# Cross attention with fast 3x3 products: setup reordered, and the last batch's softmax steps moved between engines

## The chip, the cores and the metric

The kernel runs on one core of one Trainium2 chip. The metric is the device time of one execution in microseconds. TensorE (PE in the profile) multiplies into PSUM; VectorE (DVE), ScalarE (ACT) and GpSimd (POOL) work elementwise, and only the first two of these read PSUM. SyncE (SP) issues most of the transfers. The engines run their own instruction streams, in the order that the kernel writes, and wait for one another by semaphores.

## The reference

There are 16 batches of 100 queries with 640 features, and 722 context rows of 384 features each. The first 718 rows are ordinary keys and values; the last 4 (tokens) take part in a second attention. Everything is float32 and has 8 heads of 80 features.

```python
query = hidden_states @ Wq
keyt = enc @ Wk
valt = enc @ Wv
hs = _mha(query, keyt, valt)
ca_q1 = jnp.einsum('btc,th->bch', ca, Wq_ca)[:, indices, :]
ca_hs1 = _mha(ca_q1, residual, residual)
ca_q2 = ca_hs1 @ Wq
ca_hs2 = _mha(ca_q2, ca @ Wk_ca, ca @ Wv_ca)
out = (hs + ca_hs2) @ Wout + b_out + residual
```

`_mha` scales its scores by 1/sqrt(80), takes the softmax over the keys and multiplies with the values.

## The kernel before

**Products of thirds.** The 718 keys of a batch are cut into three thirds of 240 columns (KT; two of 120, KN, for the values) and the 384 features into three channel blocks of 128 (CC). Keys and values are not made with 27 block products but with 15, from sums of encoder blocks (`enc_sums`, on GpSimd) and sums of weight blocks (`weight_sums`, twelve subtractions each for Wk and for Wv). `V_PLAN` and `K_PLAN` list the 15 products in order: the PSUM bank that takes it, its form, and the place in the result to which the bank is then added. The first bank that goes to a place is copied there by ScalarE (L412), each later one added by VectorE (L410). `go(n)` issues the next n products with their copies and adds. The last batch uses `END_PLAN`, the same products in another order.

**Setup.** Batch 0 has no earlier batch beside which its keys could be made, so `first_keys` makes them with plain products (L626): four chunks of keys times three thirds times three channel blocks, 36 products, each of which is two instructions in the profile. Ahead of them, five products on zeros (L1263) run while the first loads are under way. The weights of the keys arrive transposed (`load_heads`, L302 and L309) and are turned back by TensorE (`turn_back`, L589) and copied to `wk_sb` by VectorE or ScalarE (L592): chunks 0 and 1 at once, 2, 3 and 4 after the first four groups of products. Behind the first keys follow, in TensorE's order: the token keys k_ps (L1295), five groups of m_ps (L1319), which fold Wq into the token keys, the first queries q_ps (L544), y_ps (L805), the last chunk of the keys (L568), the other queries, and the token values va_ps (L1362). Then the loop over the batches begins with the scores s_ps (L666).

VectorE in the setup copies turned-back weights (L592), reduces a mask (L1266), makes seven of Wk's sums, all twelve of Wv's, the five late ones of Wk (these overwrite blocks of Wk that the first keys read), and then multiplies the token keys by a mask into `k2T` (L1307), which m_ps reads. It copies each group of m_ps to `m_sb` (L1327). GpSimd multiplies those by another mask (`keys`, L777) for y_ps.

**Loads.** The loads of the setup go through SyncE's queue and, for a few, ScalarE's. An issue waits until an earlier transfer has landed whose semaphore it uses again; there are eight such semaphores, taken in turn. Behind the encoder blocks stand the token loads (L319, L320), Wv (L322), Wq transposed (L326), the queries' input (L328), Wq (L333), the tokens' sample (L335) and the encoder tile of batch 1 (L248, L261).

**A batch.** A batch makes its scores in three tiles st 0, 1 and 2, each copied from PSUM by ScalarE (L688, L694), and a running maximum over the keys by VectorE (`larger`, L1403, L1412). `Maximum` turns this into one value per query and head in steps (`top.go`): transpose, reduce, four small reductions and their merge, a spread by ScalarE (L751), a transpose back (`over`, L759). `subtract` takes it from each st tile, `exponential` (L1399) follows on ScalarE. The rows of ones beside the values give the sums r_ps (L1543); a_ps (L1561) gives the values' part. The second attention runs beside it: `softmax2` (z_ps), `scores2` (three small steps on VectorE and an exponential on ScalarE), `softmax3` (two steps on VectorE, one on GpSimd), `spread2` (a transpose on VectorE, then transfers by way of DRAM: four stores L919, one widened copy L924, loads L929 and L933), and `values2` (seven steps on GpSimd, L943 and L947) with the sum `hs2`. `divide`, `place` and `finish` scale and add, and `project...` multiplies with Wout.

**The last batch.** The branch `else` of the loop body orders the last batch by hand. `last` is the batch before it, whose last full output block is projected in two halves: the first half's product early, with its sum into `xn` and its store kept back in `due` until `put()`, the second behind r_ps. r_ps reads the st tiles in the order 1, 2, 0, 1, 0, 2. The tail is `project_last` (L1225), its sum (L1234) and its store.

Of the kernel before, what the change touches and what calls it, by code (L numbers as in the profile page):

```python
# [14 lines left out]
B, S, H = 16, 100, 640  # L15
# [5 lines left out]
CC = CAD // P  # L21

KT = SK // 3 + 1
# [36 lines left out]
for h in range(NH):  # L60
    lo = h * D
    while lo < (h + 1) * D:
        c = lo // P
# [84 lines left out]
def kernel(  # L148
# [117 lines left out]
    def a_raw(enc, u, c):  # L266
        if (u, c) in A_REST:
            return enc[1][:, A_REST[u, c]]
        return enc[0][:, A_RAW[u, c]]
# [20 lines left out]
    wkt_sb = kT.rearrange("p c u k -> p c (u k)")[:, :, :CAD]  # L290
    enc = enc_tile("enc_0"), rest_tile("rest_0")

    def load_first(queue, u, lo, hi):
        to = a_raw(enc, u, lo) if hi == lo + 1 else enc[0][:, A_RAW[u, lo] :][:, : hi - lo]
        queue.dma_start(
            out=to,
            in_=enct[0][:, slice(lo, hi) if hi > lo + 1 else lo, u * (KT - 1) : u * (KT - 1) + KT],
        )

    def load_heads(u):  # L300
# [1 line left out]
            (nc.scalar, nc.sync)[h // 2 % 2].dma_start(**packed(wkt_sb, wkt, h))  # L302

    load_heads(0)
    load_first(nc.sync, 0, 0, 3)
    load_first(nc.scalar, 1, 0, 1)
    load_first(nc.sync, 1, 1, 3)
    load_heads(1)
    nc.sync.dma_start(  # L309
        out=wkt_sb[:, 4], in_=wkt.rearrange("(h k) n -> h k n", h=NH)[:, 64:]  # L310
    )
    load_first(nc.sync, 2, 0, 2)
    load_first(nc.sync, 2, 2, 3)
    tokens = pb_tile("tokens")
    beside = wide("beside")[:, : CC * (B * T + P)]
    cat_sb = beside[:, : CC * B * T].rearrange("p (c n) -> p c n", c=CC)
# [191 lines left out]
            begun = begun or first  # L508
        return begun

    def weight_sums(engine, w, late=None):

        at = lambda f: w[:, W_AT[f]]
        raw = lambda c, g: w[:, 2 * (c - 1) + g - 1]
        sums = (
            (0, raw(1, 2), raw(1, 1)),
            (11, raw(2, 2), raw(3, 2)),
            (12, raw(3, 2), raw(3, 1)),
            (5, raw(2, 2), raw(1, 2)),
            (7, raw(3, 2), at(5)),  # L520
            (13, raw(3, 1), at(7)),
            (1, raw(2, 1), raw(3, 1)),
            (3, raw(1, 1), at(7)),
            (6, raw(2, 1), raw(1, 1)),
            (10, raw(3, 1), raw(2, 2)),
            (2, raw(1, 1), raw(2, 2)),
            (14, raw(2, 1), raw(2, 2)),
        )
        for f, left, right in sums:
            if late is None or late == (f in (5, 7, 13, 3, 14)):  # L530
                engine.tensor_tensor(at(f), left, right, ALU.subtract)

# [64 lines left out]
    def first_keys(enc):  # L597

        banks = {}
        copies = nc.scalar.copy, nc.vector.tensor_copy  # L600

        def begin(n, get):
            if get is pair:
                both = pair(f"kT_ps_0_{n}")
                banks[n] = [both[:, k] for k in range(2)]
            else:
                banks[n] = [get(f"kT_ps_0_{n}_{k}") for k in range(2)]

        for n in range(2):
            turn_back(n, nc.vector.tensor_copy)  # L610
            begin(n, pair)
        for u, chunks in (
            (0, (0, 1)),
            (1, (0, 1)),
            (0, (2, 3)),
            (1, (2, 3)),
            (2, range(4)),
        ):
            if len(banks) < 4 and 2 in chunks:
                for n in (2, 3, 4):  # L620
                    turn_back(n, copies[n % 2])
                begin(2, psum1)
                begin(3, psumk)
            for n in chunks:
                for c in range(CC):
                    nc.tensor.matmul(  # L626
                        banks[n][u // 2][:, u % 2 * KT : (u % 2 + 1) * KT],
                        wk_sb[:, 2 * c + n % 2, n // 2],
                        a_raw(enc, u, c),
                        start=(u != 1 and c == 0),  # L630
                        stop=(c == CC - 1),
                        skip_group_check=True,
                    )
        for n in banks:
            for bank, thirds in zip(banks[n], ((0, 1), (2,))):
                w = len(thirds)
                nc.scalar.copy(
                    kT[:, n, thirds[0] : thirds[0] + w],
                    bank[:, : w * KT].rearrange("p (u k) -> p u k", u=w),
                )  # L640
# [618 lines left out]
    idle = vaT[:, :2].rearrange("p c n -> p (c n)")  # L1259
    nc.vector.memset(idle, 0.0)  # L1260
    idle_ps = psum("idle_ps")
    for _ in range(5):
        nc.tensor.matmul(idle_ps[:, :P], idle, idle, start=True, stop=True)  # L1263

    first_keys(enc)
# [3 lines left out]
    nc.gpsimd.memset(most[96:, :], LOW)  # L1269
    nc.gpsimd.memset(e1[96:, :], LOW)  # L1270
    weight_sums(nc.vector, wk_sb, False)
    weight_sums(nc.vector, wv_sb)
    weight_sums(nc.vector, wk_sb, True)
    enc_sums(enc)

# [40 lines left out]
    for c in range(HC):  # L1316
        m_ps = psum(f"m_ps_{c}")
        for n, heads in enumerate(HEADS):
            nc.tensor.matmul(  # L1319
                m_ps[:, heads[0] * B * T : (heads[-1] + 1) * B * T],  # L1320
                wqt_sb[:, n, c * P : (c + 1) * P],
                k2T[n],
                start=(n == 0),
                stop=(n == HC - 1),
                skip_group_check=True,
            )
        nc.vector.tensor_copy(  # L1327
            m_sb[c].rearrange("p (b h t) -> p h b t", h=NH, t=T),
            m_ps.rearrange("p (h b t) -> p h b t", h=NH, b=B),
        )  # L1330
        nc.sync.dma_start(out=m_d[c], in_=m_sb[c])
    nc.sync.dma_start(out=wvca_sb, in_=wvca.rearrange("(c p) n -> p c n", p=P))
    second = Second(0, xT, ca_0)
    keys(load_m(0))
# [38 lines left out]
    for b in range(B):  # L1373
# [16 lines left out]
        def subtract(i, engine=nc.vector):  # L1390
            return engine.tensor_tensor(  # L1391
                st[i],
                st[i],
                top.over[:KN].unsqueeze(1).to_broadcast([KN, 2, ROWS]),
                ALU.subtract,
            )
# [26 lines left out]
        if b + 1 < B:  # L1423
            second.products()
            second.copy()
        if b == B - 1:
            now.scores2()
        seen = larger(2)
        top = Maximum(most, f"{b}", True)

        if b + 1 < B:

            def both(n):
                vv.go(n)
                kk.go(n)

            if waiting:
                wait_for(enc_sums(enc, LATE_SUMS), seen)
            if waiting:
                second.scores1(tokens=range(T - 1))  # L1440
            else:
                second.scores1(seen)
            store(seen)
            if last:
                last.load(seen)
            if b == B - 2:
                again()
            if b + 2 < B:
                m_next = load_m(b + 2, seen)
            if b == 1:  # L1450
                load_outputs(nc.sync.dma_start, wout_sb, wout)
            top.go(3)
            both(3)
            now.scores2()
            top.go(1)
            both(2)
            top.go()
            both(2)
            now.softmax3()
            if waiting:  # L1460
                second.scores1(tokens=range(T - 1, T))
            if b + 2 < B:
                keys(m_next)
            both(1)
            now.spread2()
            vv.go(2)
            kk.go(1)
            subtract(0)
            exponential(0)
            vv.go(1)  # L1470
            less = subtract(1)
            if last:
                last.place(less)
                if last.b in PAIRED:
                    last.row_sums()
                last.add_bias()
            if b == B - 2:
                mine.load(seen)
            now.values2()
            if b == B - 2:  # L1480
                mine.add_bias()
            vv.go(1)
            kk.go(2)
            exponential(1)
            vv.go(1)
            kk.go(2)
            both(1)
            both(1)
            if b == 1:
                nc.gpsimd.dma_start(out=bias, in_=bout[0].partition_broadcast(P))  # L1490
            second_next, enc_next = loads()
            subtract(2)
            exponential(2)
            last_keys(b + 1, enc)
            if b + 2 < B:
                enc_next = load_rest(b + 2, enc_next)
        else:
            last.place()
            mine.load(seen)
            now.softmax3()  # L1500
            top.go(1)
            now.spread2()
            top.go(2)
            vv.go(3)
            last.project_few(len(OC) - 2)
            last.project((0,), True, put=False)
            top.go(1)
            top.go()
            vv.go(2)
            less = subtract(0)  # L1510
            exponential(0)
            wait_for(subtract(2, nc.gpsimd), less)
            vv.go(3)
            last.put()
            vv.go(1)
            now.values2(subtract(1))
            mine.add_bias()
            exponential(2)
            vv.go(1)
            exponential(1)  # L1520
            vv.go(5)
        paired = last and last.b in PAIRED
        late = b % 2 == 0 and not paired
        if b < B - 1 and (b % 2 or late):
# [106 lines left out]
```

## Time and profile before

| | before |
|---|---|
| median of 3 runs | 929.62 us (929.5 to 931.77) |
| profiled execution | 931.78 us |
| its span, first to last instruction | 930.1 us |
| PE busy | 916.3 us (99%) |
| DVE busy | 672.0 us (72%) |
| POOL busy | 616.1 us (66%) |
| ACT busy | 375.5 us (40%) |

The profiled execution's own time is 1.7 us more than its span, for what lies around the first and the last instruction. Busy time of PE counts pipelined matmuls, so 99% does not say that the array is at its peak. In a row of the order of time stand: start and length in us, engine, line, operation, output and inputs, shapes, how many instructions are merged, and in brackets the idle time before them with what ended it. In a row by windows: the stretch, its length, the busy time and count of PE, PEld, DVE, ACT and POOL, the granted TensorE clock, the DMA share and GB/s. In a row of waits: who waited for whom, the total in us, how often, and the longest.

### The profile page before, as it was taken

What the parts mean: (1) busy time and instruction counts of PE and PEld (TensorE: products, weight loads), DVE (VectorE), ACT (ScalarE), POOL (GpSimd) and SP (SyncE); (2) the same over time, 40 slices, a digit from 0 to 9 for tenths busy, and PEclk for the clock granted to TensorE, in tenths of its full rate; (3) what the DMA queues carried; (4) which work ended last, traced back from release to release, by engine and by line L of the source; (5) the groups of instructions that cost most, each with busy time, mean ns of one, the idle gap of its engine ahead of it and who ended that gap; (6) DMA issues with size and microseconds to landing.
All of it is one profiled execution on the core that took longest, in us unless ns stands there. A gap on an engine that the chain in (4) does not pass through costs nothing.

```text
span 930.1 us, 26065 instructions
## 1 busy us (share of the span) xinstructions
PE 916.3 (99%) x11151; PEld 781.3 (84%) x11151; DVE 672.0 (72%) x1122; ACT 375.5 (40%) x654; POOL 616.1 (66%) x652
## 2 busy tenths in 40 slices
PE   8899999999999999999999999999999999999998
PEld 7798979888888888888798887988888888888865
DVE  3699796887828787585966759669792887828783
ACT  1344443444424354542435324344541444415341
POOL 7455798566955778477574766846796566955623
PEclk9899999999999999999999999999999999999999
DMA  9412253051401504131141401304140141401331
GB/s 304 157 45 61 84 121 86 6 133 42 109 11 34 140 6 109 44 96 46 34 109 43 123 20 49 93 15 132 43 109 9 35 135 40 109 11 45 85 83 32
DMA packets 67997, 69.50 MB, mean 75 GB/s; under 512 B 25129, under 2 KB 61289, under 8 KB 67881
## 3 DMA queue, kind: packets, MB, share of 16 engines
q1 hardware_dynamic: 66952, 66.97, 26.8%
q8 instruction: 88, 1.44, 0.6%
q10 hardware_dynamic: 464, 0.52, 0.2%
q0 software_dynamic: 464, 0.34, 0.2%
q14 instruction: 29, 0.23, 0.1%
HBM read 62.14 MB, written 8.94 MB: 76 GB/s over the span
## 4 chain that ended last, share of the span: by engine, by line
PE 96%; DVE 2%; DMA 1%; issue 0%; POOL 0%; ACT 0%; SPq 0%; DVEq 0%
PE s_ps L666 12%; PE v_psA L439 11%; PE v_psB L439 9%; PE k_psA L470 8%; PE a_ps L1561 7%; PE q_ps L544 7%; PE k_psB L470 7%; PE kT_ps L568 6%; PE r_ps L1543 4%; PE v_psC L439 3%; PE k_psC L470 3%; PE y_ps L805 2%; PE v_psD L439 2%; PE v_psE L439 2%; PE o_psy L1134 2%; PE k_psE L470 1%
## 5 line engine op out<-in xcount | busy, mean ns | idle before, releaser
L840 POOL TENSOR_TENSOR e<-ca,g 100x800 f32<-100x800 f32 x60 | 91.7, 1539 | 102.1 <-DVE most L1403 87.9
L439 PE MATMUL v_psA<-wv_sb,enc 128*120 128x320 f32 x384 | 119.7, 434 | 0.7 <-ACT vs L412 0.7
L507 POOL TENSOR_TENSOR enc<-enc 128x240 f32<-128x240 f32 x144 | 111.6, 784 | 8.0
L439 PE MATMUL v_psB<-wv_sb,enc 128*120 128x320 f32 x320 | 99.2, 433 | 0.0
L666 PE MATMUL s_ps<-qp,kT 32*120 32x100 f32 x3072 | 97.5, 263 | 0.0
L666 PEld LDWEIGHTS s_ps<-qp,kT 32*120 32x120 f32 x3072 | 94.7, 180 | 1.9
L847 POOL TENSOR_TENSOR e<-e,e 100x800 f32<-100x800 f32 x45 | 92.1, 2047 | 3.5
L1391 DVE TENSOR_TENSOR st<-st,over 120x1600 f32<-120x1600 f32 x47 | 91.4, 1945 | 0.0
L439 PEld LDWEIGHTS v_psA<-wv_sb,enc 128*120 128x120 f32 x384 | 69.1, 184 | 25.6 <-ACT vs L412 1.2
L470 PE MATMUL k_psA<-enc,wk_sb 128*128 128x240 f32 x360 | 87.7, 366 | 0.0
L470 PEld LDWEIGHTS k_psA<-enc,wk_sb 128*128 128x128 f32 x360 | 68.6, 190 | 17.0
L1403 DVE TENSOR_TENSOR most<-most,st 120x800 f32<-120x800 f32 x64 | 63.5, 991 | 22.6 <-ACT st L688 21.5
L439 PEld LDWEIGHTS v_psB<-wv_sb,enc 128*120 128x120 f32 x320 | 58.7, 183 | 23.2
L1399 ACT ACTIVATE st<-st 120x1600 f32<-120x1600 f32 x48 | 73.9, 1540 | 7.2 <-DVE st L1391 5.2
L470 PE MATMUL k_psB<-enc,wk_sb 128*128 128x240 f32 x300 | 73.1, 366 | 0.0
L1412 DVE TENSOR_TENSOR most<-st 120x800 f32<-120x800 f32 x16 | 17.2, 1074 | 76.0 <-ACT st L694 76.0
L1561 PE MATMUL a_ps<-st,vs 120*64 120x100 f32 (+1 forms) x1536 | 69.5, 250 | 0.0
L544 PE MATMUL q_ps<-xT,wq_sb 128*128 128x200 f32 x400 | 69.1, 333 | 0.0
L1561 PEld LDWEIGHTS a_ps<-st,vs 120*64 120x64 f32 (+1 forms) x1536 | 66.4, 137 | 2.7 <-issue 2.6
L544 PEld LDWEIGHTS q_ps<-xT,wq_sb 128*128 128x128 f32 x400 | 68.0, 190 | 0.2
L412 ACT COPY vs<-v_psA 120x640 f32<-120x640 f32 x48 | 33.2, 693 | 84.4 <-PE v_psA L439 84.3
L694 ACT COPY st<-s_ps 120x800 f32<-120x800 f32 x64 | 49.7, 829 | 43.4 <-PE s_ps L666 43.4
(183 smaller groups left out, 1890.6 us busy)
## 6 DMA issues: line engine op xcount, KB each, us to landing
pb<-p_d SPq DMA_DIRECT2D x32, 400.0 KB
enc<-in_enct SPq DMA_DIRECT2D x32, 240.0 KB
enc<-in_enct SPq DMA_DIRECT2D x16, 360.0 KB
xT<-in_xt SPq DMA_DIRECT2D x8, 500.0 KB
rest<-in_enct SPq DMA_DIRECT2D x31, 120.0 KB
xn<-in_x SPq DMA_DIRECT2D x11, 320.0 KB
wide_d<-p_d SPq DMA_DIRECT2D x16, 200.0 KB
pb<-wide_d SPq DMA_DIRECT2D x16, 200.0 KB
```

The lines of the kernel that those rows point to most:

```text
L439: nc.tensor.matmul(at[0][j][:KN, : H // 2], a_form(self.enc, f)[:, j * KN : (j + 1) * KN], wv_sb[:, W_AT[f]], start=first, stop=last, skip ...
L470: nc.tensor.matmul(at[:, i * KT : (i + 1) * KT], wk_sb[:, W_AT[f], i], a_form(self.enc, f), start=(first and i == 0), stop=last, skip_grou ...
L507: first = nc.gpsimd.tensor_tensor(out, left, right, op)
L544: nc.tensor.matmul(q_ps[:, : 2 * S].rearrange("p (j s) -> p j s", j=2), wq_sb[:, c, n * P : (n + 1) * P], xT[:, :, c, :], start=(c == 0), ...
L568: nc.tensor.matmul(bank[:, i * KT : (i + 1) * KT], weights[c], a_raw(enc, u, c), start=(i == 0 and c == 0), stop=(c == CC - 1), skip_group ...
L666: nc.tensor.matmul(s_ps[bank][:n, 256 * a + lo : 256 * a + lo + rhs.shape[-1]], kT[rows, c, u, j * KN : (j + 1) * KN], rhs, start=bank not ...
L840: first = engine.tensor_tensor(to, self.ca[:, t, :].unsqueeze(1).to_broadcast([S, NH, S]), g[:, :, t].unsqueeze(2).to_broadcast([S, NH, S] ...
L847: engine.tensor_tensor(e, e, to, ALU.add)
L1391: return engine.tensor_tensor(st[i], st[i], top.over[:KN].unsqueeze(1).to_broadcast([KN, 2, ROWS]), ALU.subtract,)
L1399: nc.scalar.activation(st[i], st[i], AF.Exp, scale=SCALE)
L1403: most_now = nc.vector.tensor_tensor(most[:KN], most[:KN], st[i][:, u], ALU.max)
L1561: nc.tensor.matmul(wides[64 * e : 64 * e + 64, h // 2], slot(i, h, FIRST[e], 64), st[i // 2][: KEYS[i], i % 2, h * S : (h + 1) * S], start ...
```

## The change

- Seven products on zeros instead of five.
- The encoder blocks of batch 0 are loaded one by one, nine transfers instead of five, channel block 0 of all thirds first (one of its three by ScalarE's queue), then the rest of the transposed weights, then blocks 1 and 2. `first_keys` goes by channel blocks too: block 0 of chunks 0 and 1, then (after chunks 2, 3 and 4 are turned back) block 0 of chunks 2 and 3, then block 1 and block 2 of all four chunks.
- Wv's twelve sums stand in three places: six where all were, one behind each of the five copies of m_ps, and one after them.
- Last batch: `scores2` moves from ahead of the third tile's maximum to behind the spread; `softmax3` behind `over`; `subtract(1)` goes from VectorE to GpSimd, behind `subtract(2)`; `spread2` behind that; `values2` no longer waits for VectorE's `subtract(1)`; five value products instead of four are issued ahead of `exponential(2)`; the first half projection's sum and store (`last.put()`) go to the end.

```diff
-    load_first(nc.sync, 0, 0, 3)
-    load_first(nc.scalar, 1, 0, 1)
-    load_first(nc.sync, 1, 1, 3)
+    load_first(nc.sync, 0, 0)
+    load_first(nc.scalar, 1, 0)
+    load_first(nc.sync, 2, 0)
     load_heads(1)
...
-    load_first(nc.sync, 2, 0, 2)
-    load_first(nc.sync, 2, 2, 3)
+    for c in range(1, CC):
+        for u in range(3):
+            load_first(nc.sync, u, c)
...
-    def weight_sums(engine, w, late=None):
+    def weight_sums(engine, w, late=None, part=slice(None)):
...
-        for f, left, right in sums:
+        for f, left, right in sums[part]:
...
-        for u, chunks in (
-            (0, (0, 1)),
-            (1, (0, 1)),
-            (0, (2, 3)),
-            (1, (2, 3)),
-            (2, range(4)),
-        ):
+        for c, chunks in ((0, (0, 1)), (0, (2, 3)), (1, range(4)), (2, range(4))):
...
-                for c in range(CC):
+                for u in range(3):
                     nc.tensor.matmul(
...
-    for _ in range(5):
+    for _ in range(7):
         nc.tensor.matmul(idle_ps[:, :P], idle, idle, start=True, stop=True)
...
-    weight_sums(nc.vector, wv_sb)
+    weight_sums(nc.vector, wv_sb, part=slice(6))
     weight_sums(nc.vector, wk_sb, True)
...
         nc.sync.dma_start(out=m_d[c], in_=m_sb[c])
+        weight_sums(nc.vector, wv_sb, part=slice(6 + c, 7 + c))
+    weight_sums(nc.vector, wv_sb, part=slice(11, None))
...
-        if b == B - 1:
-            now.scores2()
         seen = larger(2)
...
             last.place()
             mine.load(seen)
-            now.softmax3()
+            top.go(3)
+            vv.go(3)
             top.go(1)
-            now.spread2()
-            top.go(2)
-            vv.go(3)
+            now.scores2()
             last.project_few(len(OC) - 2)
             last.project((0,), True, put=False)
-            top.go(1)
             top.go()
+            now.softmax3()
             vv.go(2)
             less = subtract(0)
             exponential(0)
             wait_for(subtract(2, nc.gpsimd), less)
-            vv.go(3)
-            last.put()
-            vv.go(1)
-            now.values2(subtract(1))
+            subtract(1, nc.gpsimd)
+            now.spread2()
+            now.values2()
             mine.add_bias()
+            vv.go(5)
             exponential(2)
             vv.go(1)
             exponential(1)
-            vv.go(5)
+            vv.go(4)
+            last.put()
```

More of the change, by code (lines that the diff above doesn't have):

```diff
@@ L291, with load_first @@
     enc = enc_tile("enc_0"), rest_tile("rest_0")
-    def load_first(queue, u, lo, hi):
-        to = a_raw(enc, u, lo) if hi == lo + 1 else enc[0][:, A_RAW[u, lo] :][:, : hi - lo]
+    def load_first(queue, u, c):
         queue.dma_start(
-            out=to,
-            in_=enct[0][:, slice(lo, hi) if hi > lo + 1 else lo, u * (KT - 1) : u * (KT - 1) + KT],
+            out=a_raw(enc, u, c),
+            in_=enct[0][:, c, u * (KT - 1) : u * (KT - 1) + KT],
         )
```

## The prediction

> **What bounds the kernel now.** I read the page first, then the chain that ended last, then each engine's order of time in the setup (0 to 60 us) and in the last batch (from 880 us), then the waits of the DMA queue.
>
> ```profile
> span 930.1 us, 26065 instructions
> PE 96%; DVE 2%; DMA 1%; issue 0%; POOL 0%; ACT 0%; SPq 0%; DVEq 0%
> ```
>
> TensorE carries 96% of the chain, so only the places where it stands still or runs slowly are for sale, and the changed code touches the two where it does. In the setup, TensorE (order of time: start, length, count, idle before):
>
> ```profile
> 1.13 2.51 PE L1263 MATMUL idle_ps<-vaT 128*128 128x128 f32 x10 [1.13 <-DVE vaT L1260]
> 4.58 1.51 PE L589 MATMUL w_ps<-e,kT 128*128 128x128 f32 x6 [0.94 <-DMA kT<-in_wkt]
> 7.58 5.14 PE L626 MATMUL kT_ps<-enc,wk_sb 128*128 128x240 f32 x12 [1.48 <-DMA enc<-in_enct]
> ...
> 15.42 1.15 PE L589 MATMUL w_ps<-e,kT 128*128 128x128 f32 x9
> 16.48 2.70 PE L626 MATMUL kT_ps<-enc,wk_sb 128*128 128x240 f32 x12
> ...
> 26.40 1.97 PE L1295 MATMUL k_ps<-beside,tokens 128*64 128x64 f32 x60
> 32.97 8.98 PE L1319 MATMUL m_ps<-wq,wout_sb 128*128 128x128 f32 x50 [4.60 <-DVE wq L1307]
> 41.78 1.86 PE L544 MATMUL q_ps<-xT,wq_sb 128*128 128x200 f32 x10
> ```
>
> and VectorE over the same stretch:
>
> ```profile
> 5.49 1.20 DVE L592 COPY wk_sb<-w_ps 128x384 f32<-128x384 f32 x2 [4.41 <-PE w_ps L589]
> ...
> 16.95 3.94 DVE L531 TENSOR_TENSOR wk_sb<-wk_sb 128x256 f32<-128x256 f32 x7
> 20.81 9.90 DVE L531 TENSOR_TENSOR wv_sb<-wv_sb 128x320 f32<-128x320 f32 x12
> 30.64 2.07 DVE L531 TENSOR_TENSOR wk_sb<-wk_sb 128x256 f32<-128x256 f32 x5
> 32.62 1.21 DVE L1307 TENSOR_TENSOR wq<-k_ps,hmask 128x128 f32<-128x128 f32 x5
> ...
> 40.67 0.69 DVE L1327 COPY m<-m_ps 128x512 f32<-128x512 f32 x1 [0.63 <-PE m_ps L1319]
> 41.98 0.69 DVE L1327 COPY m<-m_ps 128x512 f32<-128x512 f32 x1 [0.63 <-PE m_ps L1319]
> ```
>
> TensorE is done with k_ps at 28.37 and waits 4.60 us for VectorE, which since 16.95 has worked without a break through 24 weight sums. The 4.60 us have a second price, in the granted clock (column before the DMA share):
>
> ```profile
> 30.00:32.00 2.00, 0.00 (x0) 0.00 (x0) 1.86 (x6) 0.92 (x4) 0.00 (x0) 0.64 0.07 22
> 36.00:38.00 2.00, 2.00 (x12) 2.00 (x12) 0.62 (x1) 0.00 (x0) 0.29 (x1) 0.66 0.26 99
> ```
>
> A mean of 0.64 between full and half speed puts the fall at 30.56, 2.2 us after the last product; 0.66 puts the return at 37.36. So half of m_ps runs at half speed: 8.98 us, where the last two copies of m_ps, 1.31 us apart at full speed, give 5 x 1.31 = 6.55. The first keys too begin slowly: 5.14 us for 12 instructions, against (26.40 - 16.48)/48 = 0.207 us each later.
>
> **Setup, part by part.** Idle products: two more products are four more instructions, 4 x 0.25 = 1.0 us, from 3.64 to about 4.64. That fills the 0.94 us in which TensorE waited for the weights; it costs at most 0.06, and with it TensorE is busy without a break from 1.13 to 6.09.
>
> First loads: the first keys no longer wait for three blocks in one transfer (landed at 7.58) but for one block each. They start when the first of the two copies at 5.49 is done, about 6.1 to 6.2, if the block is there: the gain is 1.4 us, none if it is not. Product count and size are the same, 72 instructions in kT_ps. Now all three thirds of a chunk need the third channel block, and transposes 2 to 4 come after 12 instructions instead of 24, so their weights are needed sooner. Full clock from the start: 6.2 + 72 x 0.207 + 1.06 of transposes (15.42 to 16.48) = 22.2. Half clock for the first 12: 2.7 later, 24.9. I take 24.0, with a wait for the transposed weights of up to 1.6 in the first case: they go through the DMA queue, whose rows are
>
> ```profile
> 1.72 1.31 SPq L295 DMA_DIRECT2D enc<-in_enct  x2
> ...
> 11.29 5.67 SPq L333 DMA_DIRECT2D wq<-in_wq  x5
> 17.61 0.32 SPq L335 DMA_DIRECT2D ca<-in_cas  x1
> ```
>
> ```profile
> SPq L335 <- DMA wv_sb<-in_wv: 0.6, 1, 0.6
> ...
> SPq L333 <- DMA kT<-in_wkt: 0.2, 1, 0.2
> ```
>
> The queue of SP issues a load only when an earlier one has landed. L333 at 11.29 had waited for the transposed weights, so they landed then; in the new order three encoder blocks fewer are ahead of them, so I put them about 1 us earlier, 10.3. L335 at 17.61 had waited for Wv: it landed at 17.6. The change puts four more loads into SP's queue (eight blocks for four transfers), ahead of the token loads, Wv, Wq and the next encoder tile. At 0.32 (a single issue) to 0.66 (1.31/2) each and with the same bytes in flight I take 1.0 us: Wv at 18.6. Bounds: 0, and four full round trips in a row, 10.3 (priced below). The later loads have room: Wq, issued from 11.29 to 16.96, is read by q_ps, at 33 in the new order.
>
> Wv's sums: six stay ahead of Wk's late sums, five go one behind each copy of m_ps, one behind the last. The path to k2T (L1307) is the later of two. By VectorE: 18.6 + 6 x 0.83 (9.90/12) + 2.07 + 0.35 (32.62 to 32.97) = 26.0. By TensorE: Wk's late sums overwrite raw blocks that the first keys read, so 24.0 + 2.07 + 0.35 = 26.4; k_ps (1.97) runs beside them. m_ps then starts at 26.4 instead of 32.97, 6.57 sooner, and no gap is left ahead of it, so it takes 6.55 instead of 8.98: 2.43 more. Setup: 9.0 us.
>
> What is late next: VectorE gets 0.69 + 0.83 = 1.52 of work per m_ps of 1.31, and falls behind by up to 5 x 0.21 = 1.0 before the last copy, which GpSimd's mask product and y_ps wait for. q_ps, 1.86 long, lies between and covers it; without q_ps it would cost that 1.0. The twelfth sum stands ahead of the reduction of y_ps and is done by then. Everything behind moves along: the scores of the first tokens follow y_ps on VectorE as before.
>
> [...]
>
> **Last batch.** Engines in the order PE, DVE, ACT, POOL, SP:
>
> ```profile
> 902.55 1.34 PE L439 MATMUL v_psC<-wv_sb,enc 128*120 128x320 f32 x4 [0.36 <-DVE vs L410]
> ...
> 908.03 1.34 PE L439 MATMUL v_psA<-wv_sb,enc 128*120 128x320 f32 x4 [0.66 <-ACT vs L412]
> ...
> 911.61 2.28 PE L1543 MATMUL r_ps<-st,vs 120*32 120x100 f32 x96
> ...
> 920.99 5.65 PE L1225 MATMUL o_ps<-wout_sb,spare 128*128 128x480 f32 x20
> ```
>
> ```profile
> 889.29 0.60 DVE L886 TENSOR_REDUCE s<-z 100x32 f32<-100x256 f32 x1
> ...
> 890.25 2.01 DVE L1403 TENSOR_TENSOR most<-most,st 120x800 f32<-120x800 f32 x2
> ...
> 900.28 1.81 DVE L1391 TENSOR_TENSOR st<-st,over 120x1600 f32<-120x1600 f32 x1
> ...
> 904.87 2.65 DVE L1391 TENSOR_TENSOR st<-st,over 120x1600 f32<-120x1600 f32 x1
> ```
>
> ```profile
> 905.87 1.54 ACT L1399 ACTIVATE st<-st 120x1600 f32<-120x1600 f32 x1 [1.50 <-POOL st L1391]
> 907.31 0.67 ACT L412 COPY vs<-v_psA 120x640 f32<-120x640 f32 x1
> ```
>
> ```profile
> 902.24 3.59 POOL L1391 TENSOR_TENSOR st<-st,over 120x1600 f32<-120x1600 f32 x1 [9.26 <-PE v_psB L439]
> 907.65 1.03 POOL L943 TENSOR_TENSOR hs<-pb,vaT 128x500 f32<-128x500 f32 x1 [1.81 <-DVE st L1391]
> ...
> 915.59 1.54 POOL L1021 TENSOR_TENSOR spare<-spare,bias 128x640 f32<-128x640 f32 x1
> ```
>
> ```profile
> 893.59 1.72 SPq L919 DMA_DIRECT2D p_d<-p2t  x4
> ...
> 900.36 0.34 SPq L933 DMA_DIRECT2D pb<-wide_d  x1
> ```
>
> TensorE stands still twice, 0.36 and 0.66 us. The second is a copy of v_psA that sits behind the exponential of st 2 on ScalarE, which waits for GpSimd. The change sends that copy ahead of it (five value blocks before that exponential instead of four). Moving scores2 behind the maximum starts the latter 0.96 sooner (889.29 to 890.25); subtract 0 gains about 0.5 of it, since two adds ahead of it wait for products: 899.8 to 901.6. The adds of v_psE behind it go earlier too and take most of the 0.36. GpSimd then runs 901.75 to 905.35 and, with subtract 1 in place of VectorE's 2.65, to 908.95; the exponential, 1.54, ends at 910.55. r_ps reads st 1 first. TensorE without its two waits reaches r_ps at 911.61 - 1.02 = 910.6: a tie with no reserve. Gain 1.0; bounds 0.2 and 1.4.
>
> spread2 now starts behind subtract 0, at 901.6 instead of 893.59. Its transfers need 900.36 - 893.59 = 6.77 to the last issue, and about 2.3 (6.77/3, three dependent steps) to land: 910.7. GpSimd's values and bias, 907.65 to 917.13 before, then end at 920.2, their sum hs2 1.5 sooner at 918.7. The products of a_ps end near 920.0, so this hides, with 1.3 us to spare. The half projection's sum waits for nobody now; its transfer is far from the end. All behind r_ps keeps its length.
>
> **Sum.** 931.78 of the profiled execution - 9.0 - 1.0 = 921.7. That execution is 2.16 above the median of 929.62 and like the slowest run, 931.77; I predict the absolute time.
>
> **The rivals.**
> Late loads: transposed weights or Wv land 2 to 3 us later than I put them, m_ps starts near 28.5 after a gap over 2 us, and the slow clock stays. 931.78 - 4.47 - 1.0 = 926.3. For it: SP already waits on landings. Against: the transfers are the same bytes.
> GpSimd late: if each of its subtractions takes 5.0 instead of 3.59, the exponential ends at 913.3, r_ps 1.7 later than before: 931.78 - 9.0 + 1.7 = 924.5. For: the tie. Against: beside 902.24 VectorE did the same kind of adds as it will.
> The other side, slower: the four added loads do not overlap but are paid one after another, each with its issue and landing, 0.32 + 2.26 (6.77/3) = 2.58, together 10.3. Wv lands at 27.9, m_ps starts at 27.9 + 4.95 + 2.07 + 0.35 = 35.3, and the slow clock stays: 931.78 + 2.3 - 1.0 = 933.1. It decides from m_ps at 34.6 (932.4, the bound below). Against: the five issues at L333 lie 1.1 us apart (5.67/5), not 2.6. [...]
>
> **How the numbers follow.** Forecast 0.80 (m_ps at 25.0 to 27.5), late loads 0.12, GpSimd late 0.04, loads in a row 0.04. A run can be told from no change beyond 0.3%, 2.8 us: below 926.8 is faster. Forecast, GpSimd late and most late loads are: 0.94; 0.02 lies within, 0.04 above. Above 932.4 is slower. Range: low 918.8 takes m_ps at 25.0 (1.4), the last batch at its bound (0.4) and half of the 2.16; high 926.0 takes in late loads but the latest of them.
>
> **What would show it.** Right: no wait ahead of m_ps, full clock from 14 us at the latest, m_ps near 26 and 6.6 long; Wv sums between L1327 copies; r_ps a microsecond sooner and no 0.66 wait. Wrong: TensorE waiting for transposed weights before chunk 2, VectorE idle for Wv past 20 us, or r_ps waiting for the exponential of st 1.

## The result, and the profile after

| | us |
|---|---|
| after, median of 11 runs | 927.14 (925.18 to 930.39) |
| before, 11 runs on the same chip | 931.45 (929.5 to 932.25) |
| ratio, 95% interval | 0.9957 [0.9943, 0.997] |
| forecast, with its range | 921.7 (918.8 to 926.0) |
| profiled execution of after, and its span | 925.61, 923.9 |

The kernel is faster by 4.3 us, and the interval of the ratio lies wholly below 1, but it is not faster by the 10 that were forecast. The median lies 1.1 us above the range; the profiled execution lies inside it. Times vary from run to run: the profiled execution of after is the third fastest of its eleven, those of a1, a2, a3, b1, b2 and c3 below are the slowest of theirs.

The page of after (span; chain that ended last, by engine):

```profile
span 923.9 us, 26078 instructions
PE 92%; DMA 3%; DVE 2%; POOL 1%; ACT 1%; issue 0%; SPq 0%; POOLq 0%; ACTq 0%; DVEq 0%
```

TensorE's share of the chain fell from 96% to 92%: a stretch near the end has left it, and a DMA, GpSimd and VectorE carry it there. In the order of time of after, TensorE in the setup:

```profile
4.65 1.51 PE L589 MATMUL w_ps<-e,kT 128*128 128x128 f32 x6 [0.16 <-issue]
6.17 0.76 PE L620 MATMUL kT_ps<-enc,wk_sb 128*128 128x240 f32 x2
...
22.52 1.97 PE L1289 MATMUL k_ps<-beside,tokens 128*64 128x64 f32 x60 [0.24 <-ACT kT L631]
26.31 8.56 PE L1313 MATMUL m_ps<-wq,wout_sb 128*128 128x128 f32 x50 [1.82 <-DVE wq L1301]
34.70 1.86 PE L544 MATMUL q_ps<-xT,wq_sb 128*128 128x200 f32 x10
...
49.96 1.10 PE L660 MATMUL s_ps<-qp,kT 32*120 32x100 f32 x32
```

VectorE over the same stretch:

```profile
17.85 5.01 DVE L531 TENSOR_TENSOR wv_sb<-wv_sb 128x320 f32<-128x320 f32 x6 [5.09 <-DMA wv_sb<-in_wv]
22.78 3.27 DVE L531 TENSOR_TENSOR wk_sb<-wk_sb 128x256 f32<-128x256 f32 x5
25.98 1.20 DVE L1301 TENSOR_TENSOR wq<-k_ps,hmask 128x128 f32<-128x128 f32 x5
...
29.47 0.48 DVE L531 TENSOR_TENSOR wv_sb<-wv_sb 128x320 f32<-128x320 f32 x1
```

and by stretches of time (columns: stretch, its length, busy time of PE, PEld, DVE, ACT, POOL with counts, then the granted clock, DMA share, GB/s):

```profile
26.00:28.00 2.00, 1.69 (x8) 1.69 (x9) 1.18 (x6) 1.69 (x7) 0.00 (x0) 0.72 1.08 289
28.00:30.00 2.00, 2.00 (x10) 2.00 (x9) 1.09 (x2) 1.66 (x6) 0.37 (x1) 0.50 1.05 311
30.00:32.00 2.00, 2.00 (x16) 2.00 (x16) 1.05 (x2) 0.00 (x0) 0.39 (x2) 0.93 0.54 196
```

m_ps starts at 26.31, where the prediction put it. But k_ps is done at 24.49, so TensorE still stands for 1.82 us, and the clock falls all the same: 0.72 and 0.93 put the half speed between 26.87 and 30.28, 3.4 us. m_ps takes 8.56.

The last batch in after, TensorE:

```profile
879.37 0.75 PE L861 MATMUL z_ps<-y,e 100*32 100x33 f32 x64
...
902.96 2.29 PE L1537 MATMUL r_ps<-st,vs 120*32 120x100 f32 x96 [0.16 <-ACT st L1395]
...
908.06 4.35 PE L1555 MATMUL a_ps<-st,vs 120*64 120x100 f32 x96
914.58 5.65 PE L1219 MATMUL o_ps<-wout_sb,spare 128*128 128x480 f32 x20 [2.17 <-DVE spare L1092]
```

The chain that ended last in after, in the stretch in which it is off TensorE (start, length, what):

```profile
894.05 0.13 DVE p2t L910
...
896.93 3.72 DMA wide_d<-p_d
900.67 4.12 DMA pb<-wide_d
...
912.95 1.59 DVE spare L1092
```

GpSimd and then VectorE at the end of that stretch:

```profile
894.19 7.14 POOL L1387 TENSOR_TENSOR st<-st,over 120x1600 f32<-120x1600 f32 x2 [3.11 <-DVE p2t L910]
904.95 1.03 POOL L937 TENSOR_TENSOR hs<-pb,vaT 128x500 f32<-128x500 f32 x1 [3.62 <-DMA pb<-wide_d]
...
911.67 1.24 POOL L941 TENSOR_TENSOR hs<-hs,pb 128x500 f32<-128x500 f32 x1
912.87 1.53 POOL L1015 TENSOR_TENSOR spare<-spare,bias 128x640 f32<-128x640 f32 x1
```

```profile
912.95 1.57 DVE L1092 TENSOR_TENSOR spare<-spare,hs 128x100 f32<-128x100 f32 x1 [3.55 <-POOL hs L941]
```

The softmax weights of the tokens take a detour through DRAM, and their load lands 4.1 us after its issue; GpSimd waits 3.62 us for it. Its last value is ready at 912.91, half a microsecond after a_ps (912.41). Then the small sum L1092 takes 1.57 us, because GpSimd's bias sum runs beside it (0.26 without it, in b1 below), and the tail's products wait 2.17 us. In before they stood directly behind a_ps.

For the account, two more rows of before, TensorE:

```profile
57.04 1.10 PE L666 MATMUL s_ps<-qp,kT 32*120 32x100 f32 x32
...
886.91 0.75 PE L867 MATMUL z_ps<-y,e 100*32 100x33 f32 x64
```

| stretch, by starts on TensorE | before | after | difference | forecast |
|---|---|---|---|---|
| start to first scores s_ps | 57.04 | 49.96 | -7.08 | -9.0 |
| s_ps to the last batch's z_ps | 829.87 | 829.41 | -0.46 | 0 |
| z_ps to r_ps | 24.70 | 23.59 | -1.11 | -1.0 |
| r_ps to the tail's products | 9.38 | 11.62 | +2.24 | 0 |
| tail's products to the end of the span | 9.11 | 9.32 | +0.21 | 0 |
| span | 930.1 | 923.9 | -6.2 | -10.0 |

So two things are missing in this execution: 1.9 us in the setup and 2.2 us ahead of the tail. The two theories to test: the setup's loss is the clock, which falls in a gap that the prediction took for closed (rival: VectorE's longer way to k2T); the tail's loss is the landing of the token weights and the bias sum beside L1092 (rival: GpSimd's two subtractions, that is, an r_ps that comes too late).

### The profile page after: what moved, and what is told of

Its sections match the earlier page's. It is cut to its first block, busy times and chain, and to the rows that moved or that the text cites. A ratio compares the mean times of both kernels' runs of the same rounds, so it can differ in the third digit from the quotient of the medians.

```text
span 923.9 us, 26078 instructions
## 1 busy us (share of the span) xinstructions
PE 913.9 (99%) x11155; PEld 778.7 (84%) x11155; DVE 668.9 (72%) x1121; ACT 376.7 (41%) x654; POOL 622.6 (67%) x653
## 4 chain that ended last, share of the span: by engine, by line
PE 92%; DMA 3%; DVE 2%; POOL 1%; ACT 1%; issue 0%; SPq 0%; POOLq 0%; ACTq 0%; DVEq 0%
PE s_ps L660 12%; PE v_psA L439 11%; PE v_psB L439 9%; PE k_psA L470 8%; PE q_ps L544 7%; PE a_ps L1555 7%; PE k_psB L470 7%; PE kT_ps L568 6%; PE r_ps L1537 4%; PE v_psC L439 3%; PE k_psC L470 3%; PE y_ps L799 2%; PE o_psy L1128 2%; PE v_psE L439 2%; PE v_psD L439 2%; PE k_psE L470 1%
## 5 line engine op out<-in xcount | busy, mean ns | idle before, releaser
L1387 DVE TENSOR_TENSOR st<-st,over 120x1600 f32<-120x1600 f32 x46 | 88.7, 1929 | 0.0
L1399 DVE TENSOR_TENSOR most<-most,st 120x800 f32<-120x800 f32 x64 | 63.9, 998 | 23.3 <-ACT st L682 22.2
```

What stands on the lines that cost most here:

```text
L1387: return engine.tensor_tensor(st[i], st[i], top.over[:KN].unsqueeze(1).to_broadcast([KN, 2, ROWS]), ALU.subtract,)
L1399: most_now = nc.vector.tensor_tensor(most[:KN], most[:KN], st[i][:, u], ALU.max)
```

## The experiments

Each time is a median with its lowest and highest run, each ratio one to the kernel before on the same chip. The runs are from several chips, so versions are compared by their ratios.

**The two halves alone.** a1 has the setup of after and the last batch of before, a2 the reverse:

```diff
 # a1: the last batch's order of before
+            now.scores2()          # ahead of larger(2)
...
-            top.go(3)
-            vv.go(3)
+            now.softmax3()
             top.go(1)
+            now.spread2()
...
 # a2: five idle products, first loads and first keys as before
-    weight_sums(nc.vector, wv_sb, part=slice(6))
+    weight_sums(nc.vector, wv_sb)
```

> The setup as changed, the last batch as before. Theory (the change loses about 1.3 us in the last batch, because hs2 comes late): 7.1 us less than before in executions with the same granted clock, m_ps from about 26.3, and no wait ahead of the tail's products L1219 beyond a_ps. Rival (the last batch gains 1.0 as forecast and the setup gains only 5.2): 5.2 us less than before.

> The last batch as changed, the setup as before. Theory: r_ps 1.1 us sooner relative to z_ps, but the tail's products start 2.2 us after a_ps: 1.3 us more than before. Rival: 1.0 us less than before.

Measured: a1 924.21 (923.17 to 926.83), ratio 0.9937 [0.9924, 0.9951]; a2 932.14 (929.94 to 934.07), ratio 1.002 [1.001, 1.003]. TensorE in a1:

```profile
27.73 8.56 PE L1313 MATMUL m_ps<-wq,wout_sb 128*128 128x128 f32 x50 [3.19 <-DVE wq L1301]
...
915.70 5.65 PE L1219 MATMUL o_ps<-wout_sb,spare 128*128 128x480 f32 x20
```

in a2:

```profile
921.58 7.34 PE L1225 MATMUL o_ps<-wout_sb,spare 128*128 128x480 f32 x20 [3.80 <-DVE spare L1098]
```

What follows: the new last batch costs about 1.9 us (0.2% by a2, whose interval lies above 1; a1 and the whole change differ by 0.2% too, with intervals that overlap a little); the setup alone is worth 6.0, between the 7.1 and the 5.2 expected. m_ps did not start at 26.3 in a1 but at 27.73: Wv landed later, so that VectorE's sums of it began at 19.61 instead of 17.85. In a2 the tail waits 3.80 us, and in that execution the clock falls in it too, so that the tail's products take 7.34 instead of 5.65. Its load was issued at 905.82 and GpSimd's first value starts at 911.87, 6.05 us later; r_ps comes 23.56 us after z_ps (884.77), as early as in after. So the rival of a late r_ps is out.

**The token weights sent earlier.** a3 moves `spread2` ahead of the first subtraction:

```diff
             vv.go(2)
+            now.spread2()
             less = subtract(0)
             exponential(0)
             wait_for(subtract(2, nc.gpsimd), less)
             subtract(1, nc.gpsimd)
-            now.spread2()
             now.values2()
```

> The changed kernel with spread2 ahead of subtract 0, 1.8 us sooner. Theory (the landing of the widened probabilities sets hs2 and hs2 sets the tail): values2 starts 1.8 us sooner, the wait ahead of the tail's products falls from 2.17 to about 0.4 us, 1.7 us less than the changed kernel at the same granted clock. Rival (GpSimd's second subtraction sets the tail by way of r_ps): no change within 0.3 us.

Measured: 924.32 (922.34 to 927.36), ratio 0.9937 [0.9921, 0.9953]. TensorE, GpSimd and SP's queue in a3:

```profile
905.38 2.28 PE L1537 MATMUL r_ps<-st,vs 120*32 120x100 f32 x96 [0.24 <-ACT st L1395]
...
916.33 5.65 PE L1219 MATMUL o_ps<-wout_sb,spare 128*128 128x480 f32 x20 [1.50 <-DVE spare L1092]
```

```profile
906.59 1.04 POOL L937 TENSOR_TENSOR hs<-pb,vaT 128x500 f32<-128x500 f32 x1 [2.83 <-DMA pb<-wide_d]
```

```profile
900.92 0.34 SPq L927 DMA_DIRECT2D pb<-wide_d  x1
```

The time is better by 0.2%, with intervals that overlap, but the wait shrank only to 1.50, not to the 0.4 expected. Counted from r_ps the last load is issued 2.2 us sooner than in after (4.46 ahead of r_ps against 2.29), yet from its issue to GpSimd's first value it takes 5.67 us instead of 4.28 (904.95 - 900.67), so that GpSimd starts only 0.8 us sooner. L1092 is still 1.57 long.

**The bias ahead of the values.** b1 exchanges two lines, so that GpSimd adds the bias while it waits for the load:

```diff
+            mine.add_bias()
             now.values2()
-            mine.add_bias()
```

> The changed kernel with the bias sum of the last block ahead of values2 on GpSimd, where GpSimd waits for the landing anyway. Theory (VectorE's L1092, with both inputs in SBUF, stands still as long as GpSimd's bias sum runs): L1092 takes 0.26 instead of 1.57 us and the tail's products start 1.3 us sooner after hs2; 1.3 us less than the changed kernel. Rival (L1092 is long because of hs2 itself): no change.

Measured: 924.94 (923.21 to 928.34), ratio 0.9933 [0.9918, 0.9948]. VectorE and TensorE in b1:

```profile
915.33 0.26 DVE L1092 TENSOR_TENSOR spare<-spare,hs 128x100 f32<-128x100 f32 x1 [4.54 <-POOL hs L941]
```

```profile
27.40 8.56 PE L1313 MATMUL m_ps<-wq,wout_sb 128*128 128x128 f32 x50 [2.93 <-DVE wq L1301]
...
915.65 7.34 PE L1219 MATMUL o_ps<-wout_sb,spare 128*128 128x480 f32 x20 [2.03 <-DVE spare L1092]
```

The same sum with the same operands takes 0.26 instead of 1.57 once GpSimd does nothing beside it. That shows the second part of the tail's loss, 1.3 us. The time is better by 0.2%, with intervals that just overlap. The wait was 2.03 all the same in this execution, since the load landed 5.6 us after its issue (901.74 to 907.32).

**The gap filled.** a4 puts eight products on zeros between k_ps and m_ps and leaves the rest as in after:

```diff
+    between = pair("between")[:, 0]
+    for _ in range(8):
+        nc.tensor.matmul(between[:, :P], idle, idle, start=True, stop=True)
```

> The changed kernel with eight products on zeros between k_ps and m_ps. Theory (the gap of 1.82 us ahead of m_ps lets the clock fall in executions where the window falls badly): no fall ahead of m_ps, m_ps 6.6 us long, the slowest executions of the changed kernel gone, median 1.5 to 2 us less. Rival (the clock falls for another reason, or products on zeros do not hold it): m_ps still 8.5 us, median unchanged or up to 0.5 more.

Measured: 926.55 (924.3 to 927.5), ratio 0.9959 [0.9945, 0.9972]. TensorE and the stretches in a4:

```profile
26.71 6.91 PE L1316 MATMUL m_ps<-wq,wout_sb 128*128 128x128 f32 x50 [0.22 <-DVE wq L1301]
33.45 1.86 PE L544 MATMUL q_ps<-xT,wq_sb 128*128 128x200 f32 x10
...
914.87 5.65 PE L1219 MATMUL o_ps<-wout_sb,spare 128*128 128x480 f32 x20 [3.17 <-DVE spare L1092]
```

```profile
28.00:30.00 2.00, 2.00 (x17) 2.00 (x16) 1.40 (x3) 1.21 (x5) 0.47 (x1) 1.00 1.01 314
```

The mechanism is as expected: full clock, and m_ps 6.91 long although it starts 0.4 later, q_ps 1.25 sooner than in after. So 1.65 of m_ps's 8.56 us were the clock. The median does not show it: the ratio is after's, and the forecast of 1.5 to 2 us less missed. In the profiled execution the tail waits 3.17, a microsecond more than in after, and three of the six runs have a mean granted clock of 0.998: one 3.4 us stretch at half speed costs 1.7 us, which is 0.0018 of the time. That it lies in the tail's gap in those runs is only argued, since their traces were not taken; the traces of a2, b1 and b2 show a fall there.

**Five idle products instead of seven.** b2 changes one number:

```diff
-    for _ in range(7):
+    for _ in range(5):
         nc.tensor.matmul(idle_ps[:, :P], idle, idle, start=True, stop=True)
```

> The changed kernel with five products on zeros ahead of the setup instead of seven. Theory (the landing of Wv and VectorE's sums behind it set the start of m_ps, not the first keys): the first keys may run at half speed for up to 3.4 us, up to 1.7 us longer, k_ps ends up to 1.7 us later, and m_ps starts as before at 26 to 28; median within 0.5 us. Rival (the first keys set it): m_ps and the time 1 to 2 us later.

Measured: 926.12 (925.52 to 926.71), ratio 0.9943 [0.9928, 0.9957]. TensorE in b2:

```profile
10.44 0.77 PE L620 MATMUL kT_ps<-enc,wk_sb 128*128 128x240 f32 x2
...
24.77 1.97 PE L1289 MATMUL k_ps<-beside,tokens 128*64 128x64 f32 x60 [0.24 <-ACT kT L631]
27.20 6.91 PE L1313 MATMUL m_ps<-wq,wout_sb 128*128 128x128 f32 x50 [0.46 <-DVE wq L1301]
33.95 1.86 PE L544 MATMUL q_ps<-xT,wq_sb 128*128 128x200 f32 x10
```

and VectorE:

```profile
26.86 1.21 DVE L1301 TENSOR_TENSOR wq<-k_ps,hmask 128x128 f32<-128x128 f32 x5 [0.18 <-PE k_ps L1289]
```

TensorE waits 1.06 us for the first weights instead of 0.16, runs at half pace up to the pair at 10.44 (from 7.24, 0.40 us per instruction against 0.20 from 12.62) and finishes k_ps 2.25 us later. The gap ahead of m_ps is thereby 0.46, the clock holds, and q_ps starts 0.75 sooner than in after. The two products do what they are for, a fast start, but it brings the time nothing that can be told: the intervals of b2 and after overlap. In b2 the two paths to m_ps meet: VectorE's sums were done at 26.67, since Wv had landed late (its sums began at 19.15), and L1301 then waited 0.18 us for k_ps. In after it was VectorE that came last: k_ps was done 1.5 us before L1301 began.

**Fewer sums ahead of k2T.** b4 takes Wv's six sums off VectorE's path to k2T: five go to GpSimd behind its encoder sums, one more behind m_ps:

```diff
...
-    weight_sums(nc.vector, wv_sb, part=slice(6))
     weight_sums(nc.vector, wk_sb, True)
     enc_sums(enc)
+    weight_sums(nc.gpsimd, wv_sb, part=range(5))
...
-        weight_sums(nc.vector, wv_sb, part=slice(6 + c, 7 + c))
-    weight_sums(nc.vector, wv_sb, part=slice(11, None))
+        weight_sums(nc.vector, wv_sb, part=((6, 8, 9, 10, 7)[c],))
+    weight_sums(nc.vector, wv_sb, part=(5, 11))
```

> The changed kernel with no sum of Wv ahead of L1301 on VectorE: five go to GpSimd behind its encoder sums, five stay between the copies of m_ps, two behind. Theory (Wv's landing and the six sums behind it open the gap ahead of m_ps, in which the clock falls): Wk's late sums start when the first keys end, 22.3, m_ps starts near 25.2 whatever the landing, the gap is under 1 us and the clock holds; 1 to 3 us less than the changed kernel. Rival (something else, such as the token loads or the mask, holds m_ps): m_ps at 26 or later and no change.

Measured: 925.83 (925.56 to 926.42), ratio 0.9943 [0.9931, 0.9955]. TensorE, VectorE and GpSimd in b4:

```profile
26.34 6.91 PE L1313 MATMUL m_ps<-wq,wout_sb 128*128 128x128 f32 x50 [1.82 <-DVE wq L1301]
```

```profile
22.34 3.74 DVE L531 TENSOR_TENSOR wk_sb<-wk_sb 128x256 f32<-128x256 f32 x4 [9.22 <-PE kT_ps L620]
```

```profile
23.76 4.80 POOL L531 TENSOR_TENSOR wv_sb<-wv_sb 128x320 f32<-128x320 f32 x5
```

This missed: m_ps starts no sooner. Wk's late sums do start as soon as the first keys are done, but four of them now take 3.74 us, where five took 2.07 in before; GpSimd's sums run beside them from 23.76. The work moved from VectorE to GpSimd came back as longer VectorE instructions beside it. The same 1.82 us gap did not drop the clock in this execution: it is 1.00 from 24 to 34 us. The intervals of b4 and after overlap.

**The tail repaired.** c1 has the setup of after; in the last batch `scores2`, `softmax3` and `spread2` stand where before had them, the bias ahead of the values; both subtractions stay on GpSimd. b5 is the same tail with b4's setup. c2 is c1 with subtraction 1 back on VectorE:

```diff
 # c1, against after
+            now.scores2()          # ahead of larger(2), as in before
...
-            top.go(3)
-            vv.go(3)
+            now.softmax3()
             top.go(1)
-            now.scores2()
+            now.spread2()
+            top.go(2)
+            vv.go(3)
...
             subtract(1, nc.gpsimd)
-            now.spread2()
-            now.values2()
             mine.add_bias()
+            now.values2()
```

> The setup exactly as changed; in the last batch scores2, softmax3 and spread2 at their places of before, bias sum ahead of values2, and all else as changed (subtract 1 on GpSimd, five blocks ahead of the exponential, half projection's sum last). Theory (the last batch lost by the late landing and the lock alone): no wait ahead of the tail's products, 2.5 to 4 us less than the changed kernel, 6 to 8 less than before; what is left above the kernel with both edits is the clock's fall ahead of m_ps. Rival (the last batch's part is small and the setup's clock is all): within 1 us of the changed kernel.

> As the kernel with five of Wv's sums on GpSimd, and a last batch with scores2, softmax3 and spread2 at their places of before, subtract 1 still on GpSimd, the bias sum ahead of values2, five value blocks ahead of the exponential and the half projection's sum last. Theory (the last batch loses by the late landing alone, and subtract 1 on GpSimd and the order of the copies are worth the forecast 0.5 to 1): r_ps 0.5 to 1 us sooner than before relative to z_ps, no wait ahead of the tail's products, 7 to 10 us less than before in all. Rival (subtract 1 on GpSimd costs by itself): r_ps waits for the exponential and the gain over before is 6 or less.

> As c1_best_tail with subtract 1 back on VectorE, behind the adds of three value blocks. Theory (subtract 1 on GpSimd is worth little by itself, since r_ps waits for its exponential about as long as TensorE's waits were before; the copy moved ahead of the exponential is the gain): r_ps within 0.4 us of c1_best_tail relative to z_ps, time within 0.5 us. Rival (freeing VectorE is the gain): r_ps 0.6 to 1 us later and the time 0.6 to 1 us more.

| | us | ratio | z_ps to r_ps | wait ahead of the tail |
|---|---|---|---|---|
| c1 | 924.91 (922.87 to 925.78) | 0.9932 [0.9917, 0.9946] | 24.55 | 0 |
| b5 | 923.3 (922.26 to 923.86) | 0.9913 [0.99, 0.9926] | 24.00 | 0 |
| c2 | 924.79 (923.39 to 925.2) | 0.9932 [0.9918, 0.9946] | 24.09 | 0 |

TensorE in c1:

```profile
26.18 6.91 PE L1313 MATMUL m_ps<-wq,wout_sb 128*128 128x128 f32 x50 [1.83 <-DVE wq L1301]
...
902.47 2.29 PE L1539 MATMUL r_ps<-st,vs 120*32 120x100 f32 x96 [0.25 <-ACT st L1395]
...
911.86 5.65 PE L1219 MATMUL o_ps<-wout_sb,spare 128*128 128x480 f32 x20
```

and in c2:

```profile
26.80 8.56 PE L1313 MATMUL m_ps<-wq,wout_sb 128*128 128x128 f32 x50 [2.22 <-DVE wq L1301]
...
904.32 2.29 PE L1540 MATMUL r_ps<-st,vs 120*32 120x100 f32 x96
```

"The lock" in c1's expectation stands for L1092's 1.57 us beside GpSimd's bias sum, against 0.26 in b1. With the token weights sent early, nothing stands between a_ps and the tail's products in any of the three. Against before on their chips, c1 is 5.9 us faster, just short of the 6 to 8 expected, and b5 7.8, within its 7 to 10. r_ps comes 0.15 to 0.7 us sooner than in before instead of 1.1; so a part of after's gain at r_ps came from putting `scores2` and `softmax3` back, which is the same step that made the load late, and it cost more than it gave. c1 and c2 are equal: the second subtraction on GpSimd brings nothing that can be told. c1 and a1 are equal within their intervals too, so all that the change does to the last batch, once repaired, is worth too little to be told from none with this setup.

**Both gaps closed.** c3 is b5 with a4's lines, for five products:

```diff
+    between = pair("between")[:, 0]
+    for _ in range(5):
+        nc.tensor.matmul(between[:, :P], idle, idle, start=True, stop=True)
```

> The kernel with five of Wv's sums on GpSimd and the repaired last batch, with five products on zeros between k_ps and m_ps. Theory (a gap of 1.3 to 1.8 us ahead of m_ps costs the clock in some executions): no execution with the fall, median 0 to 1 us below the kernel with both edits (923.3). Rival (the gap is short enough already, the products only delay m_ps): 0 to 0.5 us more.

Measured: 921.77 (921.56 to 922.32), ratio 0.9901 [0.9884, 0.9919], the lowest of all; the interval overlaps with b5's, so the gain of the five products is not shown. TensorE in c3:

```profile
26.27 6.91 PE L1316 MATMUL m_ps<-wq,wout_sb 128*128 128x128 f32 x50 [0.54 <-DVE wq L1301]
...
911.31 5.65 PE L1219 MATMUL o_ps<-wout_sb,spare 128*128 128x480 f32 x20
```

No run of c3 has a mean granted clock below 0.999, and its runs lie within 0.8 us of one another, those of after within 5.2. The same holds of b5, whose gap ahead of m_ps, 1.27 us in its trace, has no products in it: its clock is 0.999 or 1.0 in all four runs, which lie within 1.6 us. Part of after's spread goes with the clock: its four runs with a mean of 1.0 lie within 0.8 us.

## Why the prediction was wrong, point by point

**Idle products, first loads.** Right in kind, better than forecast in size. The first keys ran at full pace from 6.8 us (0.20 us per instruction) and were done at 22.28, the forecast's lower bound of 22.2 and not its 24.0; the wait for the transposed weights that I allowed for did not come. The half clock for the first 12 instructions is not shown by the clock column, which is 1.00 from 1 to 15 us in before, after and b2; what the rows show is the pace, 5.14 us for 12 in before.

**VectorE's path to k2T.** Forecast 26.0, measured 26.3, with errors that cancelled: Wv's sums began at 17.85 instead of 18.6, six took 5.01 as forecast, Wk's late sums 3.27 instead of 2.07. The late sums grow with the time that GpSimd's sums run beside them: 2.07 with none beside (before, whose encoder sums end at 29.56), 2.56 to 2.58 with 0.6 us beside (a1, a3, b1, b2), 2.89 with 1.5 (a4, c2), 3.27 with 2.3 (after), 3.77 with 3.2 (c1). The prediction took the price without a neighbour. The close hit is luck of this execution too: with the same setup and seven products, Wv's sums began at 17.22 to 19.63 and m_ps at 26.18 to 27.73 in a1, a3, b1, c1 and c2.

**The step that failed in the setup: "no gap is left ahead of it, so it takes 6.55".** The start of m_ps, 26.4, was right to 0.1 us. But the prediction had TensorE finish k_ps at about 26.0, 0.4 us ahead of m_ps; it was done at 24.49, because the keys were faster, and the gain went into a gap of 1.82 us. m_ps took 8.56: 1.65 of the missing 2.01 is the clock (a4), 0.36 is that an undisturbed m_ps takes 6.91 (a4, b2, c3) and not 5 x 1.31. The prediction's own late-loads rival priced just this, "the slow clock stays", but tied it to loads that come late, not to keys that come early. Its own case is seen in a1 and b1, where Wv's sums began at 19.6, the gaps were 3.19 and 2.93 us, and the clock fell.

**The gap and the clock.** The prediction read from before that the clock fell 2.2 us after the last product, and its late-loads rival had a gap over 2 us cost the clock. It did fall at gaps of 2.22 (c2), 2.24 (a3) and 2.93 us (b1), but in after already at 1.82, while it held at 1.82 in b4 and 1.83 in c1.

**What is late next.** VectorE did not fall behind: a sum alone between two copies takes 0.48, not 0.83.

**r_ps a microsecond sooner, a tie.** Right: 1.11 against 1.0, with a wait of 0.16 for the exponential. GpSimd's two subtractions took 7.14, and the rival of a late GpSimd fell.

**The step that failed in the last batch: "about 2.3 (6.77/3, three dependent steps) to land ... this hides, with 1.3 us to spare".** Counted from r_ps, the way of the weights, with their transpose, began 8.9 us ahead of it (forecast 9.0), and GpSimd's values took 7.96 (forecast 8.0). The way to the first value, forecast at 9.1, took 10.9: an average over three steps priced the last one at 2.3, and from its issue to GpSimd's first value it took 4.3 us in after and 4.9 to 6.05 in a2, a3, a4, b1, b2 and b4. That used the 1.3 us of reserve and 0.5 more. The rest of the 2.17 is L1092, at 1.57 where the sum had nothing for it (0.26 in b1). In the five traces with this last batch (after, b2, a4, b4, a2) GpSimd's first value came 1.99, 2.26, 2.97, 3.02 and 3.54 us after the start of r_ps, and the tail waited 2.17, 2.41, 3.17, 3.21 and 3.80: one for one. The prediction followed GpSimd's bias sum only up to its end, and did not ask which VectorE instruction would run beside it.

**The rivals and the range.** GpSimd late and loads in a row did not occur. Of the late loads, the slow clock came without the lateness. (The sum of the forecast gives 921.78, which it put as 921.7.) The sign was right. The range failed at its upper end, and the clock is not the whole of it: the four runs of after at full clock took 925.18 to 926.0, still about 3.5 us or more above the forecast, the other seven 925.61 to 930.39. The range held a landing of 2.3 us alone. The rows quoted from before bounded it only by 7.3 (issue at 900.36, first value on GpSimd at 907.65), and a landing at that bound, with the wait that it makes ahead of the tail, belonged in the range. That the landing and falls in the tail make up the 1.5 us by which the median exceeds the profiled execution is argued from the other traces, not shown: the median run's trace was not taken.

## What to carry to other kernels

When a step speeds up the engine that waits, ask first what sets the end of the wait: the gain may only lengthen a gap, and a gap can cost the clock on top (here 1.82 us of gap, 1.65 of clock). A transfer that is moved towards the end needs a bound for its landing, taken from its own rows and not from an average over a chain, and every instruction that its consumer pushes back must be laid beside its new neighbours on the other engines (L1092 went from 0.26 to 1.57 us by one). Run each half of a two-part change alone: here one half was worth 6.0 us and the other cost 1.9.

## What the runs showed of the hardware

**The clock.** Read from stretches of 0.1 us and less, half speed (0.50) lasted in after from 26.867 to 30.280, 3.413 us, and in before from 30.546 to 37.374, twice that. In three traces with two falls, the falls lie whole steps of 3.413 us apart: b1's at 28.74 and 916.20, 260.0 steps, a2's at 31.82 and 922.70, 261.0, after's at 26.87 and 924.57 (past the last instruction), 263.0. In a4's expectation, "the window" is the stretch between two such steps.

The length of a gap alone did not decide: the clock fell at 1.82 us ahead of m_ps in after and held at 1.82 in b4 and 1.83 in c1, and it held at gaps of 3.17 us (a4) and 3.21 (b4) ahead of the tail, behind which the products took 5.65; behind b2's gap of 2.41 they took 7.34. In the 3.413 us ahead of a fall, TensorE stood still for 2.03 us or more in before, a1, a2, a3, b1 and c2 (ahead of m_ps) and in the tails of a2 and b1, and for 1.82 in after. Counted back three steps from 924.57, a step of after lies at 914.33, inside its tail's gap: 1.92 us of the gap lie ahead of it, 0.25 behind, and the clock held. What decides between 1.82 and 1.92 stays open.

**VectorE and GpSimd side by side.** L1092 takes 0.26 us in b1, where GpSimd does nothing beside it, and 1.57 in after, where it starts 0.08 us after GpSimd's 1.53 us sum and ends 0.12 us after that does. It goes the other way as well: in c2, GpSimd's bias sum took 3.14 us instead of 1.53, beside a subtraction of VectorE that had started 1.3 us sooner and ended at 900.74.

**A load of data that went through DRAM.** From the issue of the same 128-partition load of the token weights to the first value that needs it, it took 4.3 us (after), 4.9 (b2), 5.4 (a4), 5.6 (b1, b4), 5.7 (a3) and 6.05 us (a2), whether it was issued sooner or later. Why it varies stays open.
